# A graph layer on one core: addresses of copied columns from the index row itself, node features held twice, and 72 in place of 76 columns on the Vector engine

## Chip, core and metric

One core of a Trainium2 chip runs the whole program in one launch. The metric is the device time in microseconds (us); smaller is better. TensorE is called PE, VectorE DVE, ScalarE ACT, GpSimd POOL and SyncE SP, as in the profile.

## What is computed

There are 12,500 nodes with 64 features and 400,000 edges, sorted by their destination `dst`; the sources `src` are random.

```python
m_in = concatenate([x[src], x[dst], edge_attr])     # 64 + 64 + 16
h = silu(m_in @ W1 + b1)
messages = silu(h @ W2 + b2)
agg = segment_sum(messages, dst)                    # per node
y = layernorm(x + silu(concatenate([x, agg]) @ W3 + b3))
```

## The kernel before

Edges go in tiles of 128 and octets of 8 tiles: 3,125 tiles, 391 octets. One hand-ordered loop over octets `o` names every instruction of PE, ACT, DVE and SP in its order; each engine then runs its own list and waits by semaphores, so engines may stand in different octets at the same moment. POOL's gathers run beside them.

The sources' part of the first layer, x W1a, reaches PE in three ways, and a pair (two tiles, 256 edges) goes by one of them:

- **Gathers.** `gather` (L390) has POOL fetch 128 rows per instruction from a table `pa` in DRAM, up to eight per octet, three octets ahead.
- **Rows.** `rows` (L344, L348): SP reads 16 addresses per octet into registers and sends 16 small transfers. 16 octets make one pair.
- **Columns.** The transposed features lie in SBUF as `xs`. `columns` copies one edge's column of 64 partitions x 4 bytes into the tile `cx`, with an address from a register: ACT by a copy (L324), 72 per octet, DVE by a reduction over one element (L322), 40 + 36 per octet. Each run of up to eight copies follows one register load (L305), and a run ends where an edge number is a multiple of 128. From octet 12 on, 148 columns per octet fill pair after pair; a filled pair serves as one of the octet's four pairs in the first layer (L495) and needs no gathers. That makes 217 such pairs.

The register loads need byte addresses. In the kernel before, all source numbers are loaded once at octet 0 (L664, into the space of `agg`), turned into addresses 4 src + 37344 by one DVE operation (L202) and stored to a table `adr` in DRAM at octet 1 (L203). `index(o + 3)` has SP fetch 256 addresses, `cxi`, three octets ahead of a pair's first column (L375); three such rows exist at a time. Both halves of a pair read partitions 0 to 63 of `xs`; the first half writes partitions 0 to 63 of `cx`, the second 64 to 127.

DVE's list in iteration `o` is: add an older octet's window sums to the nodes, `add_window(o - 4)` (L543); compare destinations for the next octet (L466); 40 columns; up to octet 59 a window copy (L444); compare nodes for the next octet (L472); 36 columns; once in 16 octets multiply a row of 256 indices for SP's `rows` (L364); and what falls due of the node layer (L586 to L603). PE's list is: first layer of `o` (L485, L495, L498), second layer of `o - 1` (L511, L513), window sums of `o - 2` (L538), and node products that fall due (L570 to L573). ACT's list is: 72 columns of `o`, then one silu for the first layer of `o` and the second of `o - 1` (L524). SP's list is: index rows, loads of destinations and attributes (L454, L455), the window's rows of the table x W1b + b1 (L429; before octet 60 by PE from features, L433), and `rows`.

The sums of four octets share one PSUM tile `pg`, and in the trace PE's L538 starts when DVE's L543 has read it.

Of the kernel before, what the change touches and what calls it, by code (L numbers as in the profile page):

```python
# [20 lines left out]
P = 128  # L21
# [9 lines left out]
XWB = 5  # L31
TABLES = 7
ACOLS = (40, 32)
VCOLS = (40, 36)
ROWS = 16
LOADS = 8
XADDR = 37344

LAG = CT * P // 32

U = 125
# [4 lines left out]
@with_exitstack  # L46
def kernel(
    ctx: ExitStack,
    tc: tile.TileContext,
    x: bass.AP,  # L50
    xt: bass.AP,
    src_c: bass.AP,
    src_row: bass.AP,
    dst_c: bass.AP,
    dst_row: bass.AP,
    attr_t: bass.AP,
    dst_2: bass.AP,
    attr_2: bass.AP,
    base: bass.AP,
    w1: bass.AP,  # L60
    b1: bass.AP,
    w2: bass.AP,
    b2: bass.AP,
    w3: bass.AP,
    b3: bass.AP,
    out: bass.AP,
    edges: int,
):

    nc = tc.nc
    N, D = x.shape

    const = ctx.enter_context(tc.tile_pool(name="const", bufs=1))
    dram = ctx.enter_context(tc.tile_pool(name="dram", bufs=1, space=DRAM))
    pa = dram.tile([N, D], F32, name="pa")

    pw1b = dram.tile([xt.shape[1], 2 * D], F32, name="pw1b")
    badi = const.tile([1, 1], I32, name="badi")
    ident = const.tile([P, P], F32, name="ident")  # L90
    make_identity(nc, ident)

    with ExitStack() as inner:
        windows(inner, tc, ident, badi, pa, pw1b, dram, x, xt, src_c, src_row, dst_c, dst_row, attr_t, dst_2, attr_2, base, w1, b1, w2, b2, w3, b3, out, edges)

    flag = nc.values_load(badi[0:1, 0:1], min_val=0, max_val=2 * P,
                          skip_runtime_bounds_check_because="a count of partitions")
    with tc.If(flag > 0):
        general(tc, ident, x, xt, src_c, dst_c, dst_row, attr_t, w1, b1, w2, b2, w3, b3, out, edges)


def windows(ctx, tc, ident, badi, pa, pw1b, dram, x, xt, src_c, src_row, dst_c, dst_row, attr_t, dst_2, attr_2, base, w1, b1, w2, b2, w3, b3, out, edges):
    nc = tc.nc
    N, D = x.shape
    NP = xt.shape[1]
# [38 lines left out]
    XC = 2048  # L144
    xs = fast.tile([P, NP], F32, name="xs")

    def resident(c):
        w = min(XC, NP - c)
        nc.scalar.dma_start(xs[:D, c:c + w], xt[:, c:c + w])

    resident(0)
    for s in range(2):
        h = slice(s * D, (s + 1) * D)
        nc.scalar.dma_start(w2d[h, h], w2)
    resident(XC)
    w3x = const.tile([D, D], F32, name="w3x")
    b3r = const.tile([1, G, D], F32, name="b3r")

# [35 lines left out]


    agg = fast.tile([P, NP], F32, name="agg")

    adr = dram.tile([1, TILES * P], I32, name="adr")
    at = agg[:, :TILES].bitcast(I32)

    def addresses_made():
        nc.vector.tensor_scalar(at, at, 4.0, float(XADDR), op0=OP.mult, op1=OP.add)  # L202
        nc.sync.dma_start(adr.rearrange("o (p j) -> (o p) j", p=P), at)  # L203


    bf = fast.tile([1, NO], F32, name="bf")
    nc.vector.tensor_copy(bf, bi)
# [57 lines left out]
    with tc.tile_pool(name="gat", bufs=AHEAD + 2) as gat, tc.tile_pool(name="drp", bufs=2) as drp, \  # L265
# [36 lines left out]
                lo += n  # L302

        def addresses(eng, j, e0, n):
            _, regs = nc.values_load_multi_w_load_instructions(  # L305
                indices[j][0:1, e0:e0 + n], engines=(eng,), min_val=XADDR,
                max_val=XADDR + 4 * (N - 1), skip_runtime_bounds_check_because="src names a node")
            return regs

        def columns(o, eng, part):  # L310
            for j, e0, n in pieces(o, eng, part):
                regs = addresses(eng, j, e0, n)
                if pairs[j] not in cols:
                    cols[pairs[j]] = cx.tile([P, P], F32, name="cx")
                t = cols[pairs[j]].bitcast(U8)
                s = e0 // P
                h = slice(s * D, (s + 1) * D)
                for e, r in zip(range(e0 % P, e0 % P + n), regs):
                    to, frm = t[h, 4 * e:4 * e + 4], xb[:D, ds(r - XADDR, 4)]
                    if eng == ENG.DVE:  # L320

                        nc.vector.tensor_reduce(to, frm[:, :, None], AX.X, OP.max)  # L322
                    else:
                        nc.scalar.copy(to, frm)  # L324
# [46 lines left out]
        def index(o):  # L371
            for j in begun(o):
                t = cxi.tile([1, 2 * P], I32, name="cxi")
                e = octs[pairs[j]][1] * P
                nc.sync.dma_start(t, adr[:, e:e + 2 * P])  # L375
                indices[j] = t

        winrow, winreg = {}, {}
        sums = psa.tile([P, 4, S], F32, name="pg")
# [276 lines left out]
        with tc.manual_schedule(engines={ENG.PE, ENG.Activation, ENG.DVE, ENG.SP}):  # L656
            compare_dst(0)
            compare_nodes(0)
            for o in range(NO + 1):
                if o == 0:  # L660
                    sources(0, slice(CT, SCT))
                    nc.sync.dma_start(dc[:, CT:SCT], dst_c[:, CT:SCT])
                if o == 0:
                    nc.sync.dma_start(at, src_row[:, :TILES * P].rearrange("o (p j) -> (o p) j", p=P))  # L664
                for k in parts[::-1][3 * o - 3:3 * o] if o else []:
                    n = min(XC, NP - k)
                    nc.scalar.activation(agg[:, k:k + n], zero.to_broadcast([P, n]), AF.Copy)
                if o < 2:
                    for c in parts[2:5] if o == 0 else parts[5:]:
                        resident(c)  # L670
                if o == 3:
                    for s in range(2):
                        nc.scalar.dma_start(w3s[s * D:(s + 1) * D, :], w3[D:2 * D, :])
                    nc.scalar.dma_start(w3x, w3[0:D, :])
                    nc.scalar.dma_start(b3r, b3.rearrange("(o i k) -> o i k", o=1, i=1).to_broadcast([1, G, D]))
                if o == 8:
                    nc.scalar.dma_start(dc[:, SCT:], dst_c[:, SCT:])
                if o == RAW:
                    nc.vector.memset(mv, 1.0)
                    nc.vector.memset(eps, 1e-5)  # L680
                index(o + 3)
                rload(o + 3)
                if o % (SCT // OT) == 6 and (o // (SCT // OT) + 1) * SCT < TILES:
                    sources(o // (SCT // OT) + 1)
                if o + AHEAD < NO:
                    gather(o + AHEAD)
                if o + 2 < NO and octs[o + 2][3] and o + 2:
                    load(octs[o + 2][0])
                if o + 3 < NO:
                    window_load(o + 3)  # L690
                if o + 1 < min(OWN, NO):
                    window_product(o + 1)
                if o % 4 == 2:
                    bases(ENG.DVE, o - 2)
                if o >= 4:
                    add_window(o - 4)
                if o + 1 < NO:
                    compare_dst(o + 1)
                columns(o, ENG.DVE, 0)
                if o < NO:  # L700
                    first_layer(o)
                if o == 1:
                    addresses_made()
                if o == 0:
                    nc.vector.tensor_copy(b2r, b2p[:, None, :].to_broadcast([3, OT, D]))
                if o + 1 < min(OWN, NO):
                    window_copy(o + 1)
                if o + 1 < NO:
                    compare_nodes(o + 1)
                columns(o, ENG.DVE, 1)  # L710
                if o == 1:
                    relative(CT, SCT)
                if 10 <= o < 9 + len(cuts):
                    relative(cuts[o - 10], cuts[o - 9])
                if 30 <= o < 30 + 2 * LP and o % 2 == 0:
                    k = (o - 30) // 2
                    part = rel[:, k * TILES // LP:(k + 1) * TILES // LP]
                    nc.vector.tensor_reduce(lims[:, 0, k:k + 1], part, AX.X, OP.min)
                    nc.vector.tensor_reduce(lims[:, 1, k:k + 1], part, AX.X, OP.max)
                if o >= 1:  # L720
                    for c in tables[(o - 1) * per:o * per]:
                        table(c)
                if o >= 1:
                    second_layer(o - 1)
                silus(o)
                if 8 <= o < 8 + len(tables_b):
                    table_b(tables_b[o - 8])
                if o >= 2:
                    add_up(o - 2)
                raddress(o + 2)  # L730
                rows(o)
                if o < NO:
                    for f, a in todo.get(o, []):
                        f(*a)
# [292 lines left out]
```

## Time and profile before

| what | value |
|---|---|
| median of 3 runs (lowest to highest) | 3909.68 us (3902.79 to 3916.37) |
| the profiled execution: time, span | 3909.68 us, 3907.7 us |
| busy: ACT, DVE, PE, POOL | 3120.1, 2749.6, 2706.5, 2500.0 us |
| granted PE clock, mean | 0.703 |
| octets 0 to 11, 12 to 59, 60 to 390 | to about 165, 700 and 3870 us |
| DMA, mean | 62 GB/s |

In a row of groups, the columns are: line, engine, operation, output<-inputs, shape, count | busy us, mean ns of one | idle us of the engine just ahead of them and what ended it. "issue" is time in which an engine waited for nothing that the profile shows; ahead of L322 and L324 it is the register loads, which the engine's sequencer runs by itself and which are not counted as busy. Durations of neighbours overlap, so the busy total over the count is the pace of one.

### The profile page before, as it was taken

To read this page: it belongs to the slowest core of one execution; us is meant where nothing else is said; L and a number is where in the kernel's file an instruction comes from. 1 tells how busy PE (TensorE), PEld (TensorE's weight loads), DVE (VectorE), ACT (ScalarE), POOL (GpSimd) and SP (SyncE) were. 2 spreads that over 40 slices of the span, in tenths; PEclk is the share of its full clock that TensorE was granted. 3 is DMA by queue.
4 is the path that set the end of the run, shared out by engine and by line. 5 is a ranking of instruction groups with operands and counts; after the bars stand their busy time and mean duration, and the time that the engine had idled before them with its cause. 6 is when DMAs were issued, how large, how long until landed. Compare 5 with 4: busy or idle time off the path is not lost.

```text
span 3907.7 us, 116590 instructions
## 1 busy us (share of the span) xinstructions
PE 2706.5 (69%) x14985; PEld 1930.4 (49%) x14985; DVE 2749.6 (70%) x30173; ACT 3120.1 (80%) x27555; POOL 2500.0 (64%) x2654
## 2 busy tenths in 40 slices
PE   7988788667666666666666666667666666666666
PEld 5656565445444444444444444445444444444444
DVE  2367676777777777777777777777777777777775
ACT  2277777987988888878879888888798887887985
POOL 7665565766666666666666666666666666666663
PEclk7776776766666767676777766776676766776777
DMA  6322222222222222222222222222322322222222
GB/s 154 77 63 62 61 63 60 58 57 62 56 65 61 57 63 56 56 57 61 57 64 58 63 61 55 58 62 55 64 56 57 67 59 55 64 55 55 63 57 49
DMA packets 199746, 242.87 MB, mean 62 GB/s; under 512 B 86215, under 2 KB 138966, under 8 KB 198182
## 3 DMA queue, kind: packets, MB, share of 16 engines
q1 hardware_dynamic: 86660, 133.96, 14.7%
q0 software_dynamic: 84640, 86.84, 12.0%
q10 hardware_dynamic: 27650, 14.51, 1.5%
q14 instruction: 670, 5.49, 0.5%
q8 instruction: 126, 2.06, 0.2%
HBM read 220.62 MB, written 14.47 MB: 60 GB/s over the span
## 4 chain that ended last, share of the span: by engine, by line
DVE 44%; issue 20%; SPq 9%; PE 9%; DVEq 7%; ACT 6%; DMA 5%; ACTq 1%
DVE cx L322 35%; DVEq L305 7%; ACT cx L324 5%; SPq L348 5%; DVE eh L472 3%; SPq L344 2%; DVE oh L466 2%; DMA rx<-pa 2%; PE p L485 1%; PE p L513 1%; PE pg L538 1%; ACTq L305 1%; DVE agg L543 1%; PE mm L185 1%; SPq L429 1%
## 5 line engine op out<-in xcount | busy, mean ns | idle before, releaser
L390 POOL DMA_INDIRECT ga<-pa,sc x2549 | 2405.9, 944 | 1322.7 <-issue 665.6
L324 ACT COPY cx<-xs 64x4 uint8 x27052 | 2694.5, 189 | 141.0 <-issue 116.1
L322 DVE TENSOR_REDUCE cx<-xs 64x4 uint8 x28500 | 2153.1, 141 | 904.5 <-issue 834.9
L538 PE MATMUL pg<-eh,hm 128*64 128x48 f32 x6250 | 378.7, 286 | 1016.0 <-DVE agg L543 1009.3
L538 PEld LDWEIGHTS pg<-eh,hm 128*64 128x64 f32 x6250 | 319.5, 196 | 1084.6 <-DVE agg L543 1068.4
L485 PE MATMUL p<-oh,xw 128*128 128x512 f32 (+1 forms) x782 | 757.0, 1069 | 3.9 <-DVE xw L444 2.9
L524 ACT ACTIVATE hm<-p 128x1024 f32<-128x1024 f32 x389 | 397.4, 1022 | 329.8 <-PE p L513 326.5
L498 PEld LDWEIGHTS p<-ident,ga 128*128 128x128 f32 x2550 | 550.6, 303 | 153.3 <-issue 147.6
L513 PE MATMUL p<-w2d,hm 128*128 128x128 f32 x3126 | 513.6, 313 | 99.5 <-ACT hm L524 99.4
L498 PE MATMUL p<-ident,ga 128*128 128x128 f32 x2550 | 554.4, 384 | 0.0
L513 PEld LDWEIGHTS p<-w2d,hm 128*128 128x128 f32 x3126 | 436.0, 216 | 230.5 <-ACT hm L524 121.2
L466 DVE TENSOR_TENSOR oh<-dr,wrow 96x512 f32<-96x512 int32 x391 | 264.1, 675 | 29.7 <-DMA dr<-in_dst 23.7
L495 PEld LDWEIGHTS p<-cx,w1d 128*128 128x128 f32 x434 | 140.1, 323 | 211.9 <-issue 211.9
L472 DVE TENSOR_TENSOR eh<-wrow,dc 128x384 f32<-128x384 f32 x391 | 213.9, 547 | 2.2
L485 PEld LDWEIGHTS p<-oh,xw 128*128 128x128 f32 x782 | 182.4, 289 | 43.4 <-issue 10.6
L511 PE MATMUL p<-b2r,one 3*128 3x512 bf16 x391 | 189.8, 485 | 0.0
L579 ACT ACTIVATE z<-mm 128x256 f32<-128x256 f32 (+1 forms) x25 | 9.6, 384 | 209.5 <-PE mm L573 204.9
L543 DVE TENSOR_TENSOR agg<-agg,pg 128x48 f32 x391 | 79.3, 203 | 127.8 <-PE pg L538 76.9
L495 PE MATMUL p<-cx,w1d 128*128 128x128 f32 x434 | 132.1, 406 | 0.0
L390 POOL DMA_INDIRECT ga<-in_x,sc x96 | 91.9, 958 | 30.3 <-issue 27.4
L438 PE MATMUL mm<-w1bb,xr 64*96 64x128 f32 x120 | 36.9, 400 | 57.2 <-DVE xw L444 33.1
L511 PEld LDWEIGHTS <-one 3*128 3x128 bf16 x391 | 36.9, 94 | 74.4 <-issue 56.5
(91 smaller groups left out, 869.8 us busy)
## 6 DMA issues: line engine op xcount, KB each, us to landing
rx<-pa SPq DMA_DIRECT2D x5888, 0.2 KB
dr<-in_dst SPq DMA_DIRECT2D x260, 288.0 KB
ga<-pa,sc POOLq DMA_INDIRECT x2549
oh<-in_attr SPq DMA_DIRECT2D x130, 192.0 KB
xw<-pw1b SPq DMA_DIRECT2D x331, 48.0 KB
pw1b<-pbs ACTq DMA_DIRECT2D x49, 128.0 KB
cxi<-adr SPq DMA_DIRECT2D x217, 1.0 KB
xs<-in_xt ACTq DMA_DIRECT2D x6, 512.0 KB
```

The lines of the kernel that those rows point to most:

```text
L305: _, regs = nc.values_load_multi_w_load_instructions(indices[j][0:1, e0:e0 + n], engines=(eng,), min_val=XADDR, max_val=XADDR + 4 * (N - 1 ...
L322: nc.vector.tensor_reduce(to, frm[:, :, None], AX.X, OP.max)
L324: nc.scalar.copy(to, frm)
L390: nc.gpsimd.indirect_dma_start(out=ga[:, i, :], out_offset=None, in_=x if o < RAW else pa[:, :], in_offset=bass.IndirectOffsetOnAxis(ap=sc ...
L466: nc.vector.tensor_tensor(oh[:E, :], dr[:, e:e + w], wn[:E, o:o + 1].to_broadcast([E, w]), op=OP.is_equal)
L472: nc.vector.tensor_tensor(eh[:, :n], row[:, None, :].to_broadcast([P, n, S]), rel[:, t0:t0 + n, None].to_broadcast([P, n, S]), op=OP.is_equal)
L485: nc.tensor.matmul(p1[:, :k], xw[o % XWB], oh, start=True, stop=False, skip_group_check=True)
L495: nc.tensor.matmul(p1[:, 0, :], w1d, cols.pop(o), start=False, stop=False, skip_group_check=True)
L498: nc.tensor.matmul(p1[:, i, :], g2.rearrange("p s d -> p (s d)"), ident, start=False, stop=(i == k - 1), skip_group_check=True)
L513: nc.tensor.matmul(p2[:, 2 * i:2 * i + 2, :].rearrange("p s d -> p (s d)"), h[:, i, :], w2d, start=False, stop=(i == k - 1), skip_group_ch ...
L524: nc.scalar.activation(hm, pp, AF.Silu)
L538: nc.tensor.matmul(pg[s * D:(s + 1) * D, :], m[:, i, :], eh[:, i, :], start=(i < 2), stop=(i >= n - 2), skip_group_check=True)
```

## The change

- The address table is gone, with its load, its DVE operation and its store. `index` fetches 256 source numbers from the input itself. A new `address(o + 2)`, between `add_up` and `raddress` at the end of an iteration, lets DVE turn a pair's 256 numbers into addresses in place, in two operations of 128, two octets ahead of the pair's first column.
- `xs` is filled in partitions 64 to 127 too, by seven more transfers from DRAM at octets 5 to 8, and a pair's second half reads there; its addresses carry the offset 64 << 18.
- DVE makes 40 + 32 columns per octet in place of 40 + 36, so 144 per octet and 211 pairs.
- `agg` is set to zero from its front instead of from its back.

```diff
-VCOLS = (40, 36)
+VCOLS = (40, 32)
+XBASE = (0, 64 << 18)
-    def resident(c):
+    def resident(s, c):
-        nc.scalar.dma_start(xs[:D, c:c + w], xt[:, c:c + w])
+        nc.scalar.dma_start(xs[s * D:(s + 1) * D, c:c + w], xt[:, c:c + w])
-    adr = dram.tile([1, TILES * P], I32, name="adr")
-    at = agg[:, :TILES].bitcast(I32)
-    def addresses_made():
-        nc.vector.tensor_scalar(at, at, 4.0, float(XADDR), op0=OP.mult, op1=OP.add)
-        nc.sync.dma_start(adr.rearrange("o (p j) -> (o p) j", p=P), at)
...
-                    to, frm = t[h, 4 * e:4 * e + 4], xb[:D, ds(r - XADDR, 4)]
+                    to, frm = t[h, 4 * e:4 * e + 4], xb[h, ds(r - (XBASE[s] + XADDR), 4)]
...
-                nc.sync.dma_start(t, adr[:, e:e + 2 * P])
+                nc.sync.dma_start(t, src_row[:, e:e + 2 * P])
+        def address(o):
+            for j in begun(o):
+                t = indices[j]
+                for s in range(2):
+                    h = slice(s * P, (s + 1) * P)
+                    nc.vector.tensor_scalar(t[:, h], t[:, h], 4.0, float(XBASE[s] + XADDR), op0=OP.mult, op1=OP.add)
...
-                if o == 0:
-                    nc.sync.dma_start(at, src_row[:, :TILES * P].rearrange("o (p j) -> (o p) j", p=P))
-                for k in parts[::-1][3 * o - 3:3 * o] if o else []:
+                for k in parts[3 * o - 3:3 * o] if o else []:
...
+                if 5 <= o < 5 + (len(parts) + 1) // 2:
+                    for c in parts[(o - 5) * 2:(o - 4) * 2]:
+                        resident(1, c)
...
-                if o == 1:
-                    addresses_made()
...
+                address(o + 2)
                 raddress(o + 2)
```

More of the change, by code (lines that the diff above doesn't have):

```diff
@@ L93 @@
     with ExitStack() as inner:
-        windows(inner, tc, ident, badi, pa, pw1b, dram, x, xt, src_c, src_row, dst_c, dst_row, attr_t, dst_2, attr_2, base, w1, b1, w2, b2, w3, b3, out, edges)
+        windows(inner, tc, ident, badi, pa, pw1b, x, xt, src_c, src_row, dst_c, dst_row, attr_t, dst_2, attr_2, base, w1, b1, w2, b2, w3, b3, out, edges)
     flag = nc.values_load(badi[0:1, 0:1], min_val=0, max_val=2 * P,
@@ L99, with windows @@
         general(tc, ident, x, xt, src_c, dst_c, dst_row, attr_t, w1, b1, w2, b2, w3, b3, out, edges)
-def windows(ctx, tc, ident, badi, pa, pw1b, dram, x, xt, src_c, src_row, dst_c, dst_row, attr_t, dst_2, attr_2, base, w1, b1, w2, b2, w3, b3, out, edges):
+def windows(ctx, tc, ident, badi, pa, pw1b, x, xt, src_c, src_row, dst_c, dst_row, attr_t, dst_2, attr_2, base, w1, b1, w2, b2, w3, b3, out, edges):
     nc = tc.nc
@@ L145, in windows @@
     xs = fast.tile([P, NP], F32, name="xs")
-    def resident(c):
+    def resident(s, c):
         w = min(XC, NP - c)
-        nc.scalar.dma_start(xs[:D, c:c + w], xt[:, c:c + w])
-    resident(0)
+        nc.scalar.dma_start(xs[s * D:(s + 1) * D, c:c + w], xt[:, c:c + w])
+    resident(0, 0)
     for s in range(2):
@@ L154, in windows @@
         nc.scalar.dma_start(w2d[h, h], w2)
-    resident(XC)
+    resident(0, XC)
     w3x = const.tile([D, D], F32, name="w3x")
@@ L304, in addresses @@
         def addresses(eng, j, e0, n):
+            s = e0 // P
             _, regs = nc.values_load_multi_w_load_instructions(
-                indices[j][0:1, e0:e0 + n], engines=(eng,), min_val=XADDR,
-                max_val=XADDR + 4 * (N - 1), skip_runtime_bounds_check_because="src names a node")
+                indices[j][0:1, e0:e0 + n], engines=(eng,), min_val=XBASE[s] + XADDR,
+                max_val=XBASE[s] + XADDR + 4 * (N - 1), skip_runtime_bounds_check_because="src names a node")
             return regs
@@ L669, in windows @@
                     for c in parts[2:5] if o == 0 else parts[5:]:
-                        resident(c)
+                        resident(0, c)
                 if o == 3:
```

## The prediction

> **What bounds the kernel now.** I read the page first: the chain that ended last, then the costliest groups.
>
> ```profile
> DVE 44%; issue 20%; SPq 9%; PE 9%; DVEq 7%; ACT 6%; DMA 5%; ACTq 1%
> L390 POOL DMA_INDIRECT ga<-pa,sc x2549 | 2405.9, 944 | 1322.7 <-issue 665.6 <-PE p L498 597.2 <-DMA ga<-pa,sc 43.3
> L324 ACT COPY cx<-xs 64x4 uint8 x27052 | 2694.5, 189 | 141.0 <-issue 116.1 <-DMA rx<-pa 4.0 <-DVE cx L322 2.4
> L322 DVE TENSOR_REDUCE cx<-xs 64x4 uint8 x28500 | 2153.1, 141 | 904.5 <-issue 834.9 <-ACT hm L524 1.7 <-DMA rx<-pa 0.6
> ```
>
> ACT has the most busy time, but the chain runs 71% through DVE, its issue and its queue. The reductions' 904.5 us of idle time are almost all issue: register loads, which DVE's sequencer makes while the engine runs dry. POOL waited 597.2 us for PE to free its buffers, so it is ahead.
>
> Next I cut the span by stage (us; busy by engine with counts, granted clock, DMA share, GB/s), and asked for the waits and for DVE's groups in the long stage.
>
> ```profile
> 0.00:165.00 165.00, 133.62 (x650) 95.94 (x650) 33.61 (x92) 31.48 (x35) 116.80 (x129) 0.74 0.53 124
> 165.00:700.00 535.00, 436.81 (x2369) 315.16 (x2368) 366.86 (x3956) 414.93 (x3628) 321.85 (x341) 0.72 0.28 61
> 700.00:3870.00 3170.00, 2109.49 (x11778) 1499.49 (x11778) 2337.46 (x26076) 2667.79 (x23884) 2060.15 (x2184) 0.70 0.28 60
> ```
>
> ```profile
> PE pg L538 <- DVE agg L543: 1005.4, 302, 5.7
> DVE cx L322 <- issue: 729.6, 2209, 0.7
> ...
> ACT hm L524 <- PE p L513: 272.1, 172, 3.8
> ACT z L579 <- PE mm L573: 195.2, 20, 10.8
> ```
>
> ```profile
> L322 DVE TENSOR_REDUCE cx<-xs 64x4 uint8 x24807 | 1874.4, 141 | 789.1 <-issue 729.6 <-ACT hm L524 1.7 <-DMA rx<-pa 0.6
> ```
>
> Columns are PE, PEld, DVE, ACT, POOL. From 700 us on DVE is busy for 2337.5 us, and 789.1 us stand idle ahead of its reductions: 3126.6 of 3170 us. Its waits for other engines are a few us. PE waits for DVE in 302 octets of about 330, ACT waits for PE behind it. So this stage runs at DVE's pace, 3170/328 = 9.66 us per octet. ACT would need 3170 - 272 = 2898 us there by its own work. Between 165 and 700 us DVE has 366.9 us busy and 105.4 us of issue, 88% of the stretch; it is only partly the bound. Before 165 us PE is (133.6 of 165 us busy).
>
> The timeline shows one octet's end and the next one's start on DVE (start us, duration us):
>
> ```profile
> 2002.75 1.01 DVE L322 TENSOR_REDUCE cx<-xs 64x4 uint8 x12 [0.33 <-issue]
> 2003.79 0.21 DVE L543 TENSOR_TENSOR agg<-agg,pg 128x48 f32 x1
> ...
> 2008.17 0.59 DVE L322 TENSOR_REDUCE cx<-xs 64x4 uint8 x8 [0.33 <-issue]
> 2008.69 0.54 DVE L472 TENSOR_TENSOR eh<-wrow,dc 128x384 f32<-128x384 f32 x1
> ```
>
> Eight copies and the four that end the octet take 1.04 us up to the next operation; eight alone take 0.52 us.
>
> **Fewer columns and loads on DVE.** Pairs fall from 217 to 211, columns from 55,552 to 54,016: DVE has 27,000 instead of 28,500, ACT 27,016 instead of 27,052. With 148 per octet DVE's runs are 3,809, 493 of them of four copies; with 144 every boundary is a multiple of eight and 3,375 runs of eight remain. So 1,500 reductions and 434 loads go. One way: 1,500 x 75.5 ns (2153.1/28,500) = 113 us, and 434 x 237 ns (904.5/3,809) = 103 us, together 216 us. Other way: 0.52 us per octet from the timeline, x 379 octets = 197 us. By busy time alone (1.01 - 0.59 = 0.42 us) it would be 159 us. I take 200, between the two ways that count the gaps; 159 and 216 are the ends.
>
> **The address operations.** They are 422, each 1x128 int32, on DVE's path, and the trace of before has none of that shape. The nearest row is the multiplication of SP's index row, twice as wide:
>
> ```profile
> L364 DVE TENSOR_SCALAR rxi<-rxi x23: 270/281/416, 157.8 to 3635.6; 1x256 int32<-1x256 int32 x23
> ```
>
> At its mean, 302 ns, they cost 127 us; at a reduction's pace, 75.5 ns, 32 us. I take 150 ns, about half of the wide row, because in the trace neighbours overlap: 63 us. About 208 register loads at the start of a half get one more semaphore instruction, 21 ns in the trace and up to 70 ns with the gaps around it: 4 to 15 us, taken as 7. So the change adds 70 us, with ends 36 and 142. The multiplication's rows also speak on POOL: it was busy with gathers for 64% of the span (944 ns each, 300 ns between), and none of the 23 took longer than 416 ns, with 0.3 us idle ahead of all.
>
> [...]
>
> **Waits that the change adds.** The first operation of a pair waits for its index row. Queued behind it on DVE are L543, L466 and all columns; PE's L538 waits for those, and ACT for PE. SP issues the row for iteration b at the start of its iteration b - 3 (2003.39 us in the timeline, 0.40 us before DVE's L543 of that iteration), and DVE's operation stands at the end of iteration b - 2, some 18 us later: cover enough, so zero. ACT's first load of a pair now waits for DVE's operation. ACT stands about 3 us ahead: it begins the silu at 2000.72, its sequencer the next load at 2000.73, and DVE ends its octet at 2003.79. If a pair begins with ACT's first column (one in nine, as 256 j mod 144 has nine values), copies begin some 2.4 us late; ACT sat idle 1.73 us ahead of that silu anyway, and PE needs the result one octet later. Zero on the path.
>
> **The other lists.** POOL gets 12 more gathers, 12 x 1.24 = 15 us, hidden in its 597 us of waiting for PE; its octet needs about 6.8 x 1.24 = 8.4 us. SP loses two transfers of 1,562.5 KB and has 211 instead of 217 index rows; it still waits 218 us for DVE at that issue in the long stage, so it isn't late. Zeroing `agg` from its front costs what it cost from its back. ACT gains seven DMA issues (0.4 to 0.6 us) at octets 5 to 8, where it waits for PE. Their 3,157 KB replace 3,125 KB earlier on, at 0.53 DMA share; the one sensitive place is the last store of `pa`, which gathers for octet 12 wait for. They start at 133.68 us and serve a first layer at 171.57 us; one transfer of 512 KB in front costs 3.3 us at the 154 GB/s of the first slice. That cover is far wider, so zero; bare it would be those 3.3 us. DVE's operation L202 (2.0 us) lay beside PE's tables: zero. The copies of a second half read other partitions now: in the trace both halves have the same pace, 64 ns on DVE between neighbours and 95 ns on ACT, so zero.
>
> **The sum.** DVE: -200 + 70 = -130 us, ends -180 (216, 36) and -17 (159, 142). Octets 60 on are 87% of the column work and give it in full; octets 12 to 59 are 13% and I count half: 0.87 + 0.065 = 0.935, -122 us. The profiled execution took 3909.68 us, 2.0 us over its span, and is also the median: 3909.7 - 121.7 = 3788 us. The long stage should fall to about 3057 us, 9.3 us per octet, still above ACT's 2898.
>
> **Rivals.** *Another engine takes over on the way.* ACT's catching up after each node product (10 us, 20 times) and SP's 16 small transfers per octet leave DVE little slack to use. For it: ACT's 2898 us and SP's 2952 (3170 less the 218 us that it waits for DVE) are near. Against it: both lie over 100 us under the new 3057. Half the gain: -60, 3850 us. Chance 0.13.
>
> *The address work eats the gain.* If the operations cost like the wide row and the loads no more than their busy share: -17, within 0.3% (12 us) or just over: 3895 us. Chance 0.06.
>
> *Slower: DVE stands at the address operation.* Place: the first of a pair's two, 211 times, on the engine that sets the pace. Should the row or its old readers be late, all of DVE stops. It decides from 130/211 = 0.62 us per pair. The row that prices it: SP now waits 218.3 us in 93 waits for the old readers at this very issue, 2.3 us each. If DVE stood 1 us per pair, +211 - 130 = +81: 3990 us. Against it is the lead of 18 us. Chance 0.15.
>
> **The numbers.** Forecast 0.66 (3728 to 3840), other engine 0.13, both faster, and of the eaten gain a sixth: faster 0.80, same 0.05, slower 0.15. A difference of 0.3% is about what can be told from none. The range, 3728 to 3895, takes in the DVE sum's ends and the first two rivals, and leaves out the slower case and a little below.
>
> **What would show it.** Right: L322 with 27,000 reductions, under 800 us idle ahead of them, an address group of 422 near 200 ns mean and no idle time ahead, a long stage of about 3060 us, PE still waiting for L543. Wrong: idle time ahead of the address operations or of L466; DVE waiting for PE at L543; ACT waiting for the address line by hundreds of us and its silu late.

## The result, and the profile after

| | before | after |
|---|---|---|
| median (lowest to highest) | 3906.23 us (3900.97 to 3916.37) | 3783.72 us (3776.93 to 3786.62) |
| ratio, 95% interval | | 0.9681 (0.9656 to 0.9706) |
| the profiled execution: time, span | 3909.68, 3907.7 us | 3786.62, 3784.8 us |

The change makes the kernel 122.5 us faster; 3788 us were forecast. (The median of before is of four runs here, of three ahead of the prediction.) The reductions are L315 now, ACT's copies L317, the register loads L298, the address operations L376, the index row's issue L368; the other lines keep their numbers. Of the page, the chain and five groups:

```profile
PE 1%; DVE 0%; issue 0%; ACT 0%; DVEq 0%
L390 POOL DMA_INDIRECT ga<-pa,sc x2561 | 2421.4, 945 | 1180.6 <-issue 672.7
L317 ACT COPY cx<-xs 64x4 uint8 x27016 | 2701.7, 188 | 169.0 <-issue 108.4
L315 DVE TENSOR_REDUCE cx<-xs 64x4 uint8 x27000 | 2062.7, 147 | 813.1 <-issue 764.8
L524 ACT ACTIVATE hm<-p 128x1024 f32<-128x1024 f32 x389 | 396.4, 1019 | 177.8 <-PE p L513 170.8
L376 DVE TENSOR_SCALAR cxi<-cxi 1x128 int32<-1x128 int32 x422 | 80.9, 244 | 1.6
```

The chain of this execution could be followed back over one or two per cent of the span only, so it says nothing here; the waits and the stages have to carry the reading. The reductions' busy and idle time together fell from 3057.6 to 2875.8 us, 182 us, and 80.9 busy us of address operations are new, with 1.6 us idle ahead of all 422.

The waits over the whole span, and the stages (PE, PEld, DVE, ACT, POOL, granted clock, DMA share, GB/s):

```profile
PE pg L538 <- DVE agg L543: 898.7, 298, 6.6
DVE cx L315 <- issue: 764.8, 2399, 0.8
...
POOL ga L390 <- PE p L498: 443.3, 174, 13.5
```

```profile
165.00:700.00 535.00, 442.80 (x2341) 320.68 (x2339) 357.12 (x3737) 405.55 (x3549) 319.71 (x338) 0.69 0.29 61
700.00:3748.00 3048.00, 2071.90 (x11830) 1473.19 (x11830) 2311.95 (x25220) 2689.56 (x23928) 2080.64 (x2202) 0.72 0.29 62
```

PE still waits for DVE in 298 octets, POOL still waits for PE, and the only wait that the trace lists under an address operation is 4.9 us of DVE's own L543, which stands behind it. So DVE still bounds the long stage. Stages in what follows are cut at the start of the silu of octets 12, 60 and 380 in each version's trace, so that each holds the same octets:

| version (its change against before) | median us | octets 12 to 59 | octets 60 to 379 |
|---|---|---|---|
| before | 3906.23 | 520.3 | 3102.6 |
| the change | 3783.72 | 528.6 | 2973.8 |
| t72: 40 + 32 columns, table kept | 3723.01 | 526.4 | 2919.2 |
| a76: the change with 40 + 36 columns | 3958.20 | 523.1 | 3155.7 |
| s72: 36 + 36 columns, table kept | 3774.66 | 525.1 | 2970.7 |
| one72: the change, one address operation, lower reads | 3743.09 | 524.9 | 2947.5 |
| two0: the change, lower reads | 3765.03 | 526.3 | 2968.5 |
| up2: the change, all reads from above | 3802.98 | 528.5 | 2993.4 |
| d2: the change, address operations doubled | 3917.08 | 527.5 | 3102.9 |
| t72p: t72, stores on POOL | 3677.38 | 478.3 | 2921.7 |
| afterp: the change, stores on POOL | 3732.37 | 486.5 | 2971.9 |
| t64: 32 + 32 columns, table kept | 3675.44 | 530.4 | 2890.1 |
| t64p: t64, stores on POOL | 3626.42 | 465.8 | 2894.1 |
| t6464p: t64p, ACT with 32 + 32 too | 3634.90 | 471.5 | 2889.2 |

The stages come from one trace of each version. Versions that differ only in the stores agree within 4 us over octets 60 to 379 (2919.2 and 2921.7, 2973.8 and 2971.9, 2890.1 and 2894.1), so this stage repeats better than the whole time does from run to run.

The theory on trial was the prediction's sum: fewer reductions and loads on DVE gain about 187 us, address operations on DVE's path cost about 65. The rivals: address work that is hidden, an engine that takes over, and, for the parts of the sum, another cause for each.

### The profile page after: what moved, and what is told of

Same layout as the page of the kernel before. It is cut to its first block, busy times and chain, and to the rows that moved or that the text cites. A ratio compares the mean times of both kernels' runs of the same rounds, so it can differ in the third digit from the quotient of the medians.

```text
span 3784.8 us, 115732 instructions
## 1 busy us (share of the span) xinstructions
PE 2674.0 (71%) x14985; PEld 1907.6 (50%) x14985; DVE 2711.0 (72%) x29094; ACT 3132.3 (83%) x27519; POOL 2514.3 (66%) x2666
## 5 line engine op out<-in xcount | busy, mean ns | idle before, releaser
L317 ACT COPY cx<-xs 64x4 uint8 x27016 | 2701.7, 188 | 169.0 <-issue 108.4
L315 DVE TENSOR_REDUCE cx<-xs 64x4 uint8 x27000 | 2062.7, 147 | 813.1 <-issue 764.8
L538 PE MATMUL pg<-eh,hm 128*64 128x48 f32 x6250 | 367.7, 280 | 899.1 <-DVE agg L543 898.7
L538 PEld LDWEIGHTS pg<-eh,hm 128*64 128x64 f32 x6250 | 309.2, 190 | 968.4 <-DVE agg L543 958.1
L485 PE MATMUL p<-oh,xw 128*128 128x512 f32 (+1 forms) x782 | 740.9, 1047 | 0.8 <-PE pg L538 0.5
L498 PEld LDWEIGHTS p<-ident,ga 128*128 128x128 f32 x2562 | 538.4, 296 | 153.2 <-issue 150.1
L498 PE MATMUL p<-ident,ga 128*128 128x128 f32 x2562 | 541.3, 377 | 0.0
L466 DVE TENSOR_TENSOR oh<-dr,wrow 96x512 f32<-96x512 int32 x391 | 263.0, 673 | 21.4 <-DMA dr<-in_dst 21.0
L472 DVE TENSOR_TENSOR eh<-wrow,dc 128x384 f32<-128x384 f32 x391 | 213.9, 547 | 2.5
L543 DVE TENSOR_TENSOR agg<-agg,pg 128x48 f32 x391 | 78.2, 200 | 130.2 <-PE pg L538 72.1
L376 DVE TENSOR_SCALAR cxi<-cxi 1x128 int32<-1x128 int32 x422 | 80.9, 244 | 1.6
```

The lines of the kernel that those rows point to most:

```text
L466: nc.vector.tensor_tensor(oh[:E, :], dr[:, e:e + w], wn[:E, o:o + 1].to_broadcast([E, w]), op=OP.is_equal)
L472: nc.vector.tensor_tensor(eh[:, :n], row[:, None, :].to_broadcast([P, n, S]), rel[:, t0:t0 + n, None].to_broadcast([P, n, S]), op=OP.is_equal)
L485: nc.tensor.matmul(p1[:, :k], xw[o % XWB], oh, start=True, stop=False, skip_group_check=True)
L498: nc.tensor.matmul(p1[:, i, :], g2.rearrange("p s d -> p (s d)"), ident, start=False, stop=(i == k - 1), skip_group_check=True)
L538: nc.tensor.matmul(pg[s * D:(s + 1) * D, :], m[:, i, :], eh[:, i, :], start=(i < 2), stop=(i >= n - 2), skip_group_check=True)
```

## The two halves of the change apart

**t72**, the columns without the address work:

```diff
-VCOLS = (40, 36)
+VCOLS = (40, 32)
```

> The kernel before with 40 + 32 columns on DVE and nothing else: the columns' part of the change alone. If DVE's list sets the pace and costs add, 200 us leave DVE and 0.935 of it leaves the time: 3906 - 187 = 3719 us, and the difference to the changed kernel (3784) is the address work, 65 us. If the address operations lie beside other work, it is 3784 like the changed kernel. If ACT or SP takes over on the way, it stays above 3750 and PE's wait for DVE's L543 has become small.

Measured: 3723.01 us, ratio 0.9498 (0.9430 to 0.9565).

**a76**, the address work without fewer columns, made from the changed kernel:

```diff
-VCOLS = (40, 32)
+VCOLS = (40, 36)
```

> The changed kernel with 40 + 36 columns: address operations in place and features held twice, columns as before. Additive on DVE: 3906 + 70 x 0.935 = 3971 us, all of it after octet 60 but for a few us. If the address operations are hidden: 3906 us. If the second copy of the features or its transfers cost something by themselves, the time to octet 60 grows by more than 10 us.

Measured: 3958.20 us, ratio 1.0132 (1.0070 to 1.0195). The four corners are additive within 9 us: the columns bring 183 us with the table and 174 with the address work, the address work costs 52 us at 76 columns and 61 at 72. It is not hidden; without fewer columns it makes the kernel 1.3% slower, and the columns pay for it.

**s72**, the same number of columns, but runs that are not all eights: 3,750 register loads in place of 3,375.

```diff
-VCOLS = (40, 36)
+VCOLS = (36, 36)
```

> The kernel before with 36 + 36 columns: 72 copies on DVE per octet, but in 3,750 register loads (750 of them for four copies) instead of 3,375 of eight. Same copies, same pairs as with 40 + 32. If the loads stand on DVE's path, 375 more loads at 0.17 us (a load of four copies behind one of eight takes 0.69 us in place of 0.92) to 0.24 us cost 62 to 90 us of DVE and 58 to 84 us of the time over the run with 40 + 32. If they are hidden behind the copies, both times are equal.

Measured: 3774.66 us, ratio 0.9651 (0.9594 to 0.9708), 52 us over t72. The group of reductions of t72, then of s72:

```profile
L322 DVE TENSOR_REDUCE cx<-xs 64x4 uint8 x27000 | 2021.9, 141 | 841.9 <-issue 795.6
```

```profile
L322 DVE TENSOR_REDUCE cx<-xs 64x4 uint8 x27000 | 2056.6, 141 | 841.1 <-issue 759.4
```

So loads lie on the path. The idle time is the same and the busy total is 35 us higher: 375 runs more end with a copy that has no neighbour to overlap with, whose record of 141 ns counts in full where the others start every 64 ns (an estimate from these two: 375 x 77 ns = 29 us). 52 us over 375 loads is 139 ns for each, less than the 237 ns of the prediction; but two runs of four in place of one of eight have shorter loads, 0.34 us each in the trace against 0.60.

## What an address operation costs

**d2**, each address operation followed by one that multiplies its result by 1 and adds 0:

```diff
                     nc.vector.tensor_scalar(t[:, h], t[:, h], 4.0, float(XBASE[s] + XADDR), op0=OP.mult, op1=OP.add)
+                    nc.vector.tensor_scalar(t[:, h], t[:, h], 1.0, 0.0, op0=OP.mult, op1=OP.add)
```

> The changed kernel with each address operation followed by another of the same shape that multiplies by one and adds zero: 844 instead of 422. If they stand on DVE's path at the pace in the changed kernel's trace (132 ns from one to the next), 422 more cost 56 us of DVE and 52 us of the time: 3836 us. If a price per pair (the wait ahead of the first operation, ACT's wait for the last) dominates, the second set adds little: under 15 us. If each operation had to wait for POOL, hundreds.

Measured: 3917.08 us, ratio 1.0029 (0.9998 to 1.0060): 133 us more than the change, and the expectation is wrong. One pair's block in the timeline of d2:

```profile
2004.86 0.21 DVE L376 TENSOR_SCALAR cxi<-cxi 1x128 int32<-1x128 int32 x1
2005.11 0.21 DVE L377 TENSOR_SCALAR cxi<-cxi 1x128 int32<-1x128 int32 x1
2005.25 0.21 DVE L376 TENSOR_SCALAR cxi<-cxi 1x128 int32<-1x128 int32 x1
2005.49 0.22 DVE L377 TENSOR_SCALAR cxi<-cxi 1x128 int32<-1x128 int32 x1
2005.63 0.20 DVE L544 TENSOR_TENSOR agg<-agg,pg 128x48 f32 x1
```

The added operation reads what the one ahead of it has just written, and starts 0.24 to 0.25 us after it; the next, which is independent, follows after 0.14. So the block lasts 0.77 us in place of the change's 0.27. Over octets 60 to 379 this run took 129 us more than the change: by the steps from one DVE start to the next, 99 of them lie at the address operations, 7 at L543 (L544 there) and 22 at the copies that begin a run behind them. So the run did not double the cost of the change's operations, it made a chain of them; for the change itself it says that its two operations are cheap where neither waits for the other.

**one72**, one operation of 256 numbers; with it both halves read partitions 0 to 63 again, without a second copy of the features:

```diff
-                for s in range(2):
-                    h = slice(s * P, (s + 1) * P)
-                    nc.vector.tensor_scalar(t[:, h], t[:, h], 4.0, float(XBASE[s] + XADDR), op0=OP.mult, op1=OP.add)
+                nc.vector.tensor_scalar(t, t, 4.0, float(XADDR), op0=OP.mult, op1=OP.add)
...
-XBASE = (0, 64 << 18)
+XBASE = (0, 0)
```

> The changed kernel with both halves of a pair reading partitions 0 to 63 again: no second copy of the features, no offset, and one address operation of 256 numbers per pair in place of two of 128. Theory (an address block costs its instructions, about 0.27 us for two, 0.21 to 0.3 us for one wide one, and the second copy of the features costs nothing): 0 to 15 us less than the changed kernel, about 3775 us. Rival (copies that read the upper partitions are dearer, as their records of 155 ns against 139 ns might say): 27,000 copies, half of them by up to 16 ns, up to 200 us less. With columns taken from a table and no address work the time was 3723 us, so a result near that would give the whole difference to the second copy.

Measured: 3743.09 us, ratio 0.9597 (0.9559 to 0.9636): 41 us less than the change where at most 15 were expected. Two things differ, so the next two runs part them.

**two0**, two operations again, both halves still reading below (`xb[:D]`), without the second copy of the features; **up2**, the change with both halves reading above (`xb[D:]`):

```diff
-XBASE = (0, 64 << 18)
+XBASE = (0, 0)                       # two0
+XBASE = (64 << 18, 64 << 18)         # up2
```

> The changed kernel with both halves of a pair reading partitions 0 to 63 (no offset, no second copy of the features), and two address operations of 128 per pair as in the change. Between it and the kernel with one operation of 256 (3743 us) lies only the number of address operations, between it and the change (3784 us) only where the second halves read. Theory A (reading the upper partitions is dearer: in the change's trace runs of eight copies on DVE last either 595 or 621 ns, in the others all last 595): 82 ns per octet, some 30 us less than the change, near 3755 us, all runs at 595 ns. Theory B (the number of address operations costs): near 3784 us, and the runs at 595 ns without any gain.

> The changed kernel with both halves of a pair reading the upper copy, partitions 64 to 127; the first halves' writes stay in partitions 0 to 63 of cx. Theory A (a DVE copy that reads the upper partitions is dearer wherever it writes): all runs of eight last about 621 ns, some 30 us more than the change, near 3815 us. Theory A2 (only where both input and output lie in the upper half is it dearer): half of the runs at 621 ns as in the change, 3784 us. Theory B (the place costs nothing): 3784 us within 10 us, whatever the records say.

Measured: two0 3765.03 us, ratio 0.9637 (0.9605 to 0.9670); up2 3802.98 us, ratio 0.9746 (0.9707 to 0.9786). The change lies between them, 19 us from each where 30 were expected. Reading above costs something: the intervals of two0 and up2 don't overlap (that of the change overlaps two0's and ends where up2's begins), and the copies' records say it too (two0, then up2; the change has 147 ns):

```profile
L315 DVE TENSOR_REDUCE cx<-xs 64x4 uint8 x27000 | 2021.9, 141 | 845.1 <-issue 794.2 <-ACT hm L524 3.5 <-DVE cx L315 1.2
```

```profile
L315 DVE TENSOR_REDUCE cx<-xs 64x4 uint8 x27000 | 2108.9, 155 | 735.2 <-issue 661.7 <-ACT hm L524 3.4 <-DVE oh L466 0.6
```

But most of a longer record is taken back: busy rises by 87 us, idle falls by 110. In the change's trace the next run's load begins 220 ns after the last copy's start, and the median from that start to the next run's is 464 ns after an upper read as after a lower one. What is left shows in the change's timeline, where a run of eight goes over into L472, once in a first half and once in a second:

```profile
2006.49 0.59 DVE L315 TENSOR_REDUCE cx<-xs 64x4 uint8 x8 [0.32 <-issue]
2007.01 0.54 DVE L472 TENSOR_TENSOR eh<-wrow,dc 128x384 f32<-128x384 f32 x1
...
2017.25 0.62 DVE L315 TENSOR_REDUCE cx<-xs 64x4 uint8 x8 [0.29 <-issue]
2017.88 0.56 DVE L472 TENSOR_TENSOR eh<-wrow,dc 128x384 f32<-128x384 f32 x1
```

In the first half L472 starts 0.52 us after the run's start, while the copies still end; in the second it starts 0.63 us after, when the last copy is done (15 ns behind its end in the mean). Over the trace the step from the last copy to L472 is 64 ns after a first half and 180 ns after a second. In the kernel before it had two values already, 64 and 154 ns; there the second half wrote above but read below. The change adds 26 ns: copies that read above have records that grow along a run of eight, to 166 ns for the eighth, where the eighth of a lower read takes 138. In up2 the step is long in every octet (177 and 180 ns). Why L472 starts so late behind these copies, no run shows. Over octets 60 to 379 the change takes 5 us more than two0, and 4 of them lie at the steps into L472. up2 takes 20 us more than the change: its steps into L472, into the address operations and into the copies behind L472 and L466 are 66 us longer, and at later runs of an octet 41 are taken back. The medians give 19 and 19.

From t72 over octets 60 to 379 the address work now falls into three: one wide operation +28 us (180 pairs, 0.16 us each), a second operation +21, upper reads +5. These are differences of single traces; by the whole times one72 and the change differ, but two0 can't be told from either. By the steps from one DVE start to the next, the change's 55 us over t72 lie at the address operations (42), at L543 behind them (6), at L472 (4) and at copies that begin a run, so behind a later register load (4).

## Why octets 12 to 59 gained nothing

The prediction counted half of the gain there, 8.5 us; the stage grew by 8 us in the change and by 6 in t72. In both traces ACT stands at the issue of the store of `pw1b` (L416), which is in its own list after L415, and its next columns are queued behind. The change's timeline on ACT:

```profile
379.91 0.24 ACT L415 COPY pbs<-mm 128x128 f32<-128x128 f32 x1
383.09 0.38 ACTq L416 DMA_DIRECT2D pw1b<-pbs  x1
```

The copy ends at 380.15 us and the issue begins at 383.09. Over the 49 stores the time from the copy's end to the issue sums to 60 us before, 67 in the change, 66 in t72: in 16 to 19 octets 1 to 6 us, in most of the others 0.03 us. **t72p** and **afterp** have the store issued by POOL:

```diff
-                nc.scalar.dma_start(pw1b[c:c + n, :].rearrange("(i p) d -> p i d", p=P), t)
+                nc.gpsimd.dma_start(pw1b[c:c + n, :].rearrange("(i p) d -> p i d", p=P), t)
```

> The kernel before with VCOLS = (40, 32), and the stores of the table x W1b + b1 for octets 12 to 59 issued on POOL's queue instead of ACT's. In the traces so far ACT stands some 60 us in all at the issue of those stores, and octets 12 to 59 take 520 to 529 us whatever DVE does there. Theory (ACT's wait at that issue holds these octets): they fall from 526 us by 40 to 60 us, and the kernel from about 3720 to about 3670 us. Rival (the store isn't what holds them; PE, DVE and ACT wait for one another at the window copy): they stay at 526 us and the kernel within 10 us of 3720. Third (POOL has to stand at the issue in ACT's place and gathers come late): longer than 526 us.

> The changed kernel with the stores of x W1b + b1 for octets 12 to 59 on POOL's queue. With 40 + 32 columns from a table this took 48 us out of octets 12 to 59 (526 to 478 us). Theory (there ACT's wait at the issue set the pace, so DVE's savings could bring nothing): 40 to 50 us less than the change, near 3738 us, these octets about 480 us. Rival (the change's later start of octet 12 and its own address work hold them): less than 20 us.

Measured: t72p 3677.38 us, ratio 0.9443 (0.9404 to 0.9481); afterp 3732.37 us, ratio 0.9562 (0.9540 to 0.9584). Octets 12 to 59 fall by 48 and 42 us, the later octets stay. ACT's wait there, from 165 to 640 us, in the kernel before, in the change and in afterp:

```profile
ACT cx L324 <- issue: 95.1, 55, 6.9
```

```profile
ACT cx L317 <- issue: 74.4, 51, 6.5
```

```profile
ACT pbs L415 <- DMA pw1b<-pbs: 19.6, 7, 9.1
ACT cx L317 <- issue: 15.4, 51, 0.5
```

So ACT's wait at this store was the bound of the stage, and DVE's savings could not shorten it. The next section's runs agree: with the store on ACT the step from 72 to 64 columns leaves the stage at 526 and 530 us, with the store on POOL it goes from 478 to 466. What the issue itself waits for, the profile doesn't name; that stays open.

## How far fewer columns go

**t64** has 32 + 32 columns on DVE with the table, **t64p** the stores on POOL besides, **t6464p** 32 + 32 on ACT too:

```diff
-VCOLS = (40, 36)
+VCOLS = (32, 32)
-ACOLS = (40, 32)          # t6464p alone
+ACOLS = (32, 32)
```

> The kernel before with VCOLS = (32, 32): 136 columns per octet, 199 pairs, on DVE 23,944 copies in 2,993 loads. By DVE's work alone the octets 60 to 380 would take 0.1 us a copy and 0.2 us a load less per octet, some 8.2 us against 9.12 with 40 + 32, about 300 us less and a time near 3430 us. Rival from the prediction (another engine becomes the bound): ACT's own work there is 8.84 us per octet, SP's transfers and POOL's gathers lie near 8.5 to 9; then an octet takes 8.9 to 9.1 us, the stage 2850 to 2910 us, and the kernel 3650 to 3720 us, with PE waiting for ACT or for gathers instead of DVE.

> As with 32 + 32 columns on DVE, and the stores of octets 12 to 59 on POOL's queue. Theory (ACT's wait at the store's issue holds octets 12 to 59): 40 to 70 us less than with the stores on ACT. Rival: the same time within 10 us.

> The kernel before with 32 + 32 columns on ACT and on DVE, stores on POOL's queue: 128 columns per octet, 188 pairs, 11 pairs more to be gathered. Going from 40 + 32 to 32 + 32 on DVE alone brought only 28 us of the 320 octets' 2922, so another engine bounds them. If that is ACT (its own work 8.84 us per octet), eight copies less are 0.77 us plus a load less: down by some 100 to 250 us from 3626. If it is SP with its 16 small transfers per octet (the destinations' loads, behind them on SP, now come late: 253 us), nothing: 3626 within 15 us, and the waits for those loads grow. If POOL is it, longer by the 88 more gathers, 100 us.

Measured: t64 3675.44 us (ratio 0.9416, 0.9364 to 0.9468), t64p 3626.42 us (0.9300, 0.9263 to 0.9336), t6464p 3634.90 us (0.9309, 0.9288 to 0.9330). Octets 60 to 379 take 9.03 to 9.04 us each, 28 to 29 us less in all than with 72 columns, where by the expectation DVE's work alone would have given some 300. So another engine takes over right behind 72 columns. It isn't ACT: eight copies less per octet on it change 5 us. POOL seems not to be it either, since it still waits 165 us for PE; this is weaker, because 11 pairs less mean 22 more gathers (27 us at 1.24 us each), not the 88 of the expectation. The chain of t6464p, which could be followed here:

```profile
SPq 26%; PE 18%; DMA 15%; DVE 15%; issue 14%; POOL 5%; ACT 4%; DVEq 2%; ACTq 1%; POOLq 0%
SPq L348 15%; DVE cx L322 10%; SPq L344 6%; POOL ga L390 5%; PE p L485 5%; DMA dr<-in_dst 5%; ACT cx L324 4%; DMA oh<-in_attr 3%; PE p L498 3%; PE p L513 3%; DMA rx<-pa 3%; SPq L429 3%; DMA xw<-pw1b 2%; PE pg L538 2%; DVEq L305 2%
```

SP's register loads and small transfers lead, and DVE waits 168 us in it for the destinations' load (`oh` L466 for `dr`), PE 185 us for the attributes'. SP in turn hardly waits: at the index row's issue it stands 56 us for ACT and DVE in t64p, 353 us in the kernel before. That points at SP, and the prediction's own figure for SP's work, 2952 us over 328 octets, is 9.0 us each. It is not shown: the expected growth of the first wait didn't come (253 us in t64p), and no run took work from SP. t64p is the fastest version of this study, 157 us under the change.

## The prediction, point by point

- **DVE sets the pace from octet 60 on: right.** Fewer columns took 183.4 us out of 320 octets, 0.573 us each.
- **The columns' 200 us: a little small there.** 0.573 us x 379 octets is 217 us, which is the prediction's first way (216); s72 shows that the price of a load in it depends on the run's length; the timeline's 0.52 us per octet was the poorer row, because it holds one load less for an octet, where 434 loads over 379 octets are 1.15.
- **Half of the gain in octets 12 to 59: wrong.** Zero came. The prediction read DVE's 88% there as half a bound, and missed ACT's wait at the store, which stands in the kernel before as 95.1 us of issue between 165 and 640 us. The two errors cancel: of the forecast 187 us the prediction put 174 behind octet 60 and 13 ahead of it; in t72's trace 190 us came behind octet 60 and 6 were lost in octets 12 to 59. That the total, 183 us by the medians, came so near is luck.
- **The address work's 70 us, 65 after the factor: right in size** (61 us at 72 columns, 52 at 76). The mean record of 244 ns is 1.6 times the 150 ns taken for one, but neighbours overlap: from one start to the next it is 0.13 us inside a pair. The second cause, the later register loads, was priced at 7 us; the steps to copies that begin a run are 4 us longer in the change than in t72 over octets 60 to 379. The later step at L472, another 4 us, was not in the sum.
- **POOL beside the address operations: some records are longer.** The prediction read of L364 that none of its 23 records exceeded 416 ns while POOL was busy for 64% of the span, and added nothing to the operations for POOL. In the change 100 of the 422 operations begin 0.51 to 0.78 us after a gather's start. Their records average 350 ns, the longest 470, and 95 of them end 0.98 to 1.06 us after that start, just behind the gather's own end at 0.94. The other 322 average 211 ns and none exceeds 288. A longer pair beside its gather, and then one that isn't longer:

```profile
989.89 0.94 POOL L390 DMA_INDIRECT ga<-pa,sc  x1 [0.30 <-issue]
990.40 0.54 DVE L376 TENSOR_SCALAR cxi<-cxi 1x128 int32<-1x128 int32 x2
...
2010.73 0.34 DVE L376 TENSOR_SCALAR cxi<-cxi 1x128 int32<-1x128 int32 x2
```

In the prediction's own row, L364, the five longest of 23 (367 to 416 ns) began 0.64 to 0.69 us after a gather's start and ended 1.05 us after it, so the longest records of that row show the same. The reductions show nothing alike: their mean is 147 or 148 ns in every tenth of a microsecond of a gather. So beside a gather the records of these operations are longer by at most 0.27 us (470 ns against 203 of the shortest), and only in part of its time; by 14 us in all. What makes them longer, no run shows, and how much of it reaches DVE's pace is open.

- **No new waits: right.** 1.6 us idle ahead of the address operations rules the slower rival out; POOL still waits 443 us for PE. Octet 12's silu starts at 168 to 180 us in the five versions that hold the features twice and at 165 to 184 in the nine others, so no cost of the second copy's transfers shows. Two of the signs were narrowly missed: 813 us idle ahead of the reductions where under 800 was asked, and 244 ns for an address operation where near 200 was.
- **Reading other partitions at the same pace, so zero: not quite.** Inside a run the starts keep the same pace, 64 ns, but its end is 26 ns later: 5 us by the stage, 19 by the medians, and nothing here settles which. The prediction looked at neighbours in a run and not at what follows the run.
- **Another engine takes over: wrong for this change, right for the next.** It happens at 9.03 us per octet; the change stands at 9.29.

## What to carry to other kernels

Price work on the bounding engine with its gaps, not by its busy share: instructions times busy per instruction plus loads times idle per load came out right here where that engine was the bound (216 us, 217 measured). Before a saving is counted in a stage, find the wait that ends last in that stage; a DMA issue in a compute engine's own list can hold it with no engine named, as ACT's store did here, up to 5.9 us at one issue. A row's longest records deserve a look at what runs beside them before they are taken as a bound. And two edits in one change deserve their own prices: here one gained 183 us and the other gave 61 back.

## What was not expected of the hardware

- A DVE operation on 128 numbers that reads what the one ahead of it wrote starts 0.24 us after it (d2), an independent one 0.13 to 0.14 (the change, d2).
- DVE copies of 64 x 4 bytes that read partitions 64 to 127 have records of 155 ns in place of 141 (up2, before), though they start every 64 ns alike; ACT's are shorter, 187 in place of 189 ns.
- Of the change's 100 DVE operations on one partition's 128 numbers that began 0.51 to 0.78 us after the start of a gather on POOL, 95 ended 0.98 to 1.06 us after it, just behind the gather's end at 0.94, with records of up to 470 ns; those that began at other moments took at most 288.
